# One more block on seven products, and three pieces of work moved to other engines, in a fused transformer layer on one core

## The chip, the cores and the metric

The kernel runs on one core of one Trainium2 chip. A core has a matrix engine (PE, or TensorE), three engines for element-wise work (DVE or VectorE, ACT or ScalarE, POOL or GpSimd) and queues that start transfers (SP, and one on each of the other engines). Each engine takes its own instructions strictly in the order in which they were written; where an instruction needs something from another engine, it waits on a semaphore, and everything behind it on its own engine waits too. The metric is the device time of one execution in microseconds; lower is better.

## The reference

One transformer layer without dropout, in float32, for two sequences (B = 2) of S = 1024 tokens of width D = 256, with a context of T = 154 rows of width 192 for each sequence:

```
h = layernorm(x, ln1);  x = attention(h, h) + x            # 16 heads of 64
h = layernorm(x, ln2);  x = attention(h, context) + x      # 16 heads of 64
h = layernorm(x, ln3)
p = h @ ff_w1 + ff_b1                                      # 256 -> 2 * 1024
a, gate = p[..., :1024], p[..., 1024:]
h = a * gelu(gate) @ ff_w2 + ff_b2                         # 1024 -> 256
return h + x
```

Only the last four lines, the gated layer, and the third layernorm are touched by the change.

## The kernel before

**The gated layer in blocks.** After the self attention (loop over `p`) and the cross attention (loop over `c`), a last loop over `k` runs the gated layer. The 2048 tokens are cut into `NPR` = 4 blocks ("pairs" in the code) of 512: blocks 0 and 1 are the first sequence, 2 and 3 the second. For each block the first projection is made in `NF` = 8 pieces of 128 hidden features, and each piece takes two steps: `gate_first` (even `k`) and `gate_second` (odd `k`), with a remainder, `gate_last`, that is issued inside the next `gate_first`. So block 0 is made in steps 0 to 15, block 1 in 16 to 31, block 2 in 32 to 47, block 3 in 48 to 63. The pieces are numbered n = k // 2.

**The first projection** is written as seven products in place of eight (a Strassen-Winograd scheme for 2x2 blocks), with sums of weights (`weight_sums`) and sums of tokens (`token_sums`) made on GpSimd beforehand. In each piece, PE makes 7 products of 128x256 into the PSUM tiles `pa`, `pb`, `pc`; ScalarE copies `pa` to `own[:, 0]` (L1097), VectorE adds it to the others (L1101, L1103, L1117, L1120, L1129), ScalarE makes the two GELUs (L1115, L1121), and GpSimd multiplies value and gate into `ub`, the two hidden tiles of a block (L1122, L1131; 256 tokens each, called j = 1 and j = 0). `pa` is written twice: by product 1 in `gate_first` and, accumulating, by product 2 in `gate_second`, which may not start before ScalarE has copied the first value out (L1097).

**The second projection** has two forms. Blocks in `FAST`, which is 1 to 3, take seven products too: `quick_tokens` makes sums of the hidden values (4 operations of 128x128 for each pair of feature pieces and each j, 32 a block, L1194 to L1197), `quick_weights` makes four sums of the second weight (128x512 each, L1179 to L1182), and `fast_sum` is one of the seven products, 4 matrix products of 128x128 for each j (L1217). Block 0 takes `sum_slot` instead: 32 plain matrix products of 128x256 (L1247). Either way the work goes into the list `sums`, from which each step of the loop takes two plain products or one `fast_sum`; the sums of hidden values go into the list `combos`, from which each step takes two. Results are added to the tokens `x` by VectorE (L1231, L1257; the first of the seven products also by GpSimd, L1226) and then stored to `out` by DMA.

**Where the sums live.** `hold_quick` takes the tile `quick` in the place of a big attention tile that the cross attention still reads until step 5. Before, it is called in step 18, with the weight sums put at the head of `combos`.

**The third layernorm of the second sequence** (`norm_beside("ff", B - 1)`, from step 7) runs beside the gated layer of the first: for each pair of token tiles, VectorE makes mean and variance (L242, L243), GpSimd makes `var` and `rstd` (L248, L252: `deviation`), VectorE makes `off` = -mean * rstd (L258), GpSimd writes the normalized tiles `xn` (L273), PE turns them (L286), and ScalarE writes them to `hT` (L301). There are four such pairs of tiles. Their tokens are not needed before block 2.

**The order** is written out by hand, piece by piece; the lines of one step of the loop stand in this order:

```
(gate_second if k % 2 else gate_first)(k // 2)      # 7 products a piece, with gate_last
...
fn, n = sums.pop(0)                                 # second projection, 2 or 1 a step
...
for _ in range(min(2, len(combos))): combos.pop(0)[1]()
run_work(0 if k == 1 else 1 + k % 2, k % 2)         # a step of the norm
```

Of the kernel before, what the change touches and what calls it, by code (L numbers as in the profile page):

```python
# [18 lines left out]
def tile_transformer_block(ctx: ExitStack, tc: tile.TileContext, a: dict, out: bass.AP):  # L19
    nc = tc.nc  # L20
# [3 lines left out]
    B, S, D = x.shape  # L24
# [27 lines left out]
    NF = DF // P  # L52
# [9 lines left out]
    small = ctx.enter_context(tc.tile_pool(name="small", bufs=4))  # L62
# [35 lines left out]
    for n in names:  # L98
        k = n_of[n]
# [68 lines left out]
    for n in names[2:]:  # L168
        own = rows[row_of[n] - n_cols:row_of[n] - n_cols + n_of[n], :]
# [53 lines left out]
    def norm_pieces(kind, b, first=False):  # L223

        ln = {"sa": "ln1", "ca": "ln2", "ff": "ln3"}[kind]
        g0, b0 = row_of[ln + "_g"], row_of[ln + "_b"]  # L230
        st = {}
        nh = NC if kind == "ff" else NH
        order = tile_order(kind)

        def stats(t):
            if t == 0:
                st["hT"] = hT[kind, b] = p2.tile(
                    [P, nh, NC * S // nh], F32, tag="hT", name=f"hT_{ln}_{b}")
            if t % 2 == 0:
                st["mv", t] = small.tile([P, 2, 2], F32, tag="mv", name=f"mv_{ln}_{b}_{t}")  # L240
            s6 = small.tile([P, 6], F32, tag="st", name=f"st_{ln}_{b}_{t}")
            nc.vector.bn_stats(s6, xt[b, order[t] // GT][:, order[t] % GT, :])  # L242
            nc.vector.bn_aggr(st["mv", t // 2 * 2][:, t % 2, :], s6)  # L243

        def deviation(t):
            mv = st["mv", t]
            var = small.tile([P, 2], F32, tag="var", name=f"var_{ln}_{b}_{t}")
            (nc.vector if first else nc.gpsimd).tensor_scalar(  # L248
                var, mv[:, :, 1], EPS, 1.0, op0=ALU.add, op1=ALU.mult
            )  # L250
            rstd = small.tile([P, 2], F32, tag="rstd", name=f"rstd_{ln}_{b}_{t}")
            nc.gpsimd.tensor_tensor(rstd, var, power, ALU.pow)  # L252
            st["rstd", t] = rstd

        def normalize(t):
            rstd = st["rstd", t]
            off = small.tile([P, 2], F32, tag="off", name=f"off_{ln}_{b}_{t}")
            nc.vector.scalar_tensor_tensor(  # L258
                off, st["mv", t][:, :, 0], -1.0, rstd, op0=ALU.mult, op1=ALU.mult
            )  # L260
            if narrow(kind, b) and not first:
                xn = st["hT"][:, :, t * P // 2:(t + 2) * P // 2].rearrange(
                    "p c (i d) -> p c i d", i=2)
                st["xn", t] = [xn[:, c].rearrange("p i d -> p (i d)") for c in range(nh)]
            else:
                xn = pp_.tile([P, nh, 2, D // nh], F32, tag="P", name=f"xn_{ln}_{b}_{t}")
                flat = xn.rearrange("p c i d -> p (c i d)")
                st["xn", t] = [flat[:, i * P:(i + 1) * P] for i in range(2 * D // P)]
            for i in range(2):
                xs = xt[b, order[t + i] // GT][:, order[t + i] % GT, :]  # L270
                xs, own = xs.rearrange("p (c d) -> p c d", c=nh), xn[:, :, i, :]
                if not narrow(kind, b) or first and i == 1:
                    nc.gpsimd.tensor_scalar(  # L273
                        own, xs, rstd[:, i:i + 1], off[:, i:i + 1], op0=ALU.mult, op1=ALU.add)
                else:
                    nc.scalar.activation(
                        own, xs, AF.Identity, bias=off[:, i:i + 1], scale=rstd[:, i:i + 1])

        def turn(t):

            n = 2 if first else 1
            bank = mm_tile if first and t == 2 else spare["bank"]
            ph = [bank(f"ph_{ln}_{b}_{t}_{i}") for i in range(n)]
            for i in range(2 * D // P):

                nc.tensor.transpose(  # L286
                    ph[i * n * P // (2 * D)][:, i % (2 * D // P // n) * P:][:, :P],
                    st["xn", t][i], ident)

            def store():  # L290
                k = NC * 2 * P // nh
                for c in range(nh):
                    own = st["hT"][:, c, t // 2 * k:(t // 2 + 1) * k]
                    turned = ph[c * n // nh][:, c % (nh // n) * k:][:, :k]
                    gain, shift = cols[:, g0 + c:g0 + c + 1], cols[:, b0 + c:b0 + c + 1]
                    if spare["turned"] or first and c < nh // 2:
                        nc.vector.tensor_scalar(
                            own, turned, gain, shift, op0=ALU.mult, op1=ALU.add
                        )
                    else:  # L300
                        nc.scalar.activation(own, turned, AF.Identity, bias=shift, scale=gain)  # L301

            return store

        return (
            [lambda t=t: stats(t) for t in range(NT)],
            *([lambda t=t, f=f: f(t) for t in range(0, NT, 2)] for f in (deviation, normalize, turn)),
        )

    def tile_order(kind):  # L310

        if kind == "ff":
# [457 lines left out]
    CG = [(t, min(TG, NT - t)) for t in range(0, NT, TG)]  # L770
# [224 lines left out]
    NPR = B * 2  # L995
    BT = S // 4
    FU = NPR * NF
    wsum, wh, ub, psum, pools = {}, {}, {}, {}, {}
# [144 lines left out]
                (lambda i=i, e=e: sum_slot(pair, i, e), 1) for i in range(2 * TF) for e in range(NF))  # L1143

    sums, summed, quick, combos, mixed = [], {}, {}, [], {}
    FAST = range(1, NPR)
    NHF = NF // 2

    def hold_quick():
# [22 lines left out]
    def quick_weights():  # L1172

        (b11, b12), (b21, b22) = (
            [w2[:, h::2, d * P:(d + 1) * P] for d in range(2)] for h in range(2))
        t1, t2, t3, t4 = (quick["w", i] for i in (1, 2, 3, 4))
        tt = nc.gpsimd.tensor_tensor
        return [
            lambda: tt(t1, b12, b11, ALU.subtract),  # L1179
            lambda: tt(t2, b22, t1, ALU.subtract),  # L1180
            lambda: tt(t3, b22, b12, ALU.subtract),
            lambda: tt(t4, b21, t2, ALU.subtract),  # L1182
        ]

    def quick_tokens(pair, j, c, engine=nc.gpsimd):

        u, own = ub[pair][j], quick["u", (2 * pair + j) % 4]
        (a11, a12), (a21, a22) = (
            [u[:, 2 * c + h, e * P:(e + 1) * P] for h in range(2)] for e in range(2))
        s1, s2, s4 = (own[:, i, c, :] for i in range(3))  # L1190
        tt = engine.tensor_tensor
        mixed[pair, j] = mixed.get((pair, j), 0) + 1
        return [
            lambda: tt(s1, a21, a22, ALU.add),  # L1194
            lambda: tt(s2, s1, a11, ALU.subtract),
            lambda: tt(a21, a11, a21, ALU.subtract),
            lambda: tt(s4, a12, s2, ALU.subtract),  # L1197
        ]

    def fast_sum(pair, j, g):  # L1200
# [63 lines left out]
    with tc.manual_schedule():  # L1264
# [59 lines left out]
        for p in range(SA):  # L1324
# [28 lines left out]
            if hg == LAG:  # L1353
                f = (ui - NPAIR // 2 - 1) * EC
# [108 lines left out]
        for k in range(2 * FU):  # L1463
            c = CA + k
            if k == 0:
                run_work(0, 0, n_sum=2)
            flush(adds)
            (gate_second if k % 2 else gate_first)(k // 2)
            flush(stores)
            flush(lates)  # L1470
            if k == 2 * len(CG) + 1:
                norm_beside("ff", B - 1)
            cross_drain(c)
            if k % 2:
                cross_weigh(c - 1 if k == len(CG) + 2 else c)
            cross_regroup(c)
            if k == len(CG) + 2:
                out_pieces("ca", B - 1, NQ - 1, out_order("ca"))
            if k % (2 * NF) == NF and k < 2 * FU - 2 * NF:
                token_sums(k // (2 * NF) + 1)  # L1480
            n_left = 2
            while n_left > 0 and sums:
                fn, n = sums.pop(0)
                n_left -= n
                run(fn)
            flush(stores)
            if k == 2 * NF + 2:
                hold_quick()
                combos[:0] = [(None, fn) for fn in quick_weights()]
            for _ in range(min(2, len(combos))):  # L1490
                combos.pop(0)[1]()
            run_work(0 if k == 1 else 1 + k % 2, k % 2)
            if later and (k <= len(CG) + 2 or k > 2 * NF):
                if k <= len(CG) + 2 or k % 2:
                    later.pop(0)()
# [39 lines left out]
```

## Time and profile before

| | us |
|---|---|
| time, median of 3 runs | 1072.13 (1070.64 to 1073.63) |
| the profiled execution, its own time | 1075.05 |
| its span, first to last instruction | 1073.2 |
| PE busy in the span | 1059.4 (99%) |
| VectorE, ScalarE, GpSimd busy in the span | 883.1, 646.9, 777.0 |
| first product of the gated layer starts at | 900.79 |

The profile is of one execution. A busy PE is not a PE at its peak: matrix products are pipelined, and their ends are modelled, so the distance from one start to the next says what a product costs. In float32 a matrix product shows as two records; "x4" of the plain second projection is two products. Times in the views are microseconds from the start of the span. A line such as L1097 is line 1097 of the kernel before.

### The profile page before, as it was taken

What the parts mean: (1) busy time and instruction counts of PE and PEld (TensorE: products, weight loads), DVE (VectorE), ACT (ScalarE), POOL (GpSimd) and SP (SyncE); (2) the same over time, 40 slices, a digit from 0 to 9 for tenths busy, and PEclk for the clock granted to TensorE, in tenths of its full rate; (3) what the DMA queues carried; (4) which work ended last, traced back from release to release, by engine and by line L of the source; (5) the groups of instructions that cost most, each with busy time, mean ns of one, the idle gap of its engine ahead of it and who ended that gap; (6) DMA issues with size and microseconds to landing.
All of it is one profiled execution on the core that took longest, in us unless ns stands there. A gap on an engine that the chain in (4) does not pass through costs nothing.

```text
span 1073.2 us, 48628 instructions
## 1 busy us (share of the span) xinstructions
PE 1059.4 (99%) x20196; PEld 716.2 (67%) x20196; DVE 883.1 (82%) x1321; ACT 646.9 (60%) x2096; POOL 777.0 (72%) x1652
## 2 busy tenths in 40 slices
PE   8999999999999999999999999999999999999998
PEld 6566777556556555555665665466766667788998
DVE  5789899998989989999999899968777887655554
ACT  5766677677666666676777666665566564342231
POOL 2677777778777777677777777776666876499884
PEclk9999999999999999999999999999999999999999
DMA  3132122121021121111111101125776545000000
GB/s 101 38 73 54 29 68 53 25 63 41 22 59 25 34 51 34 39 34 34 44 22 45 44 14 38 36 59 139 164 177 172 123 108 114 16 6 15 21 10 30
DMA packets 86045, 60.95 MB, mean 57 GB/s; under 512 B 32122, under 2 KB 74562, under 8 KB 85826
## 3 DMA queue, kind: packets, MB, share of 16 engines
q1 hardware_dynamic: 84450, 57.07, 22.1%
q8 instruction: 159, 2.61, 1.1%
q10 hardware_dynamic: 1376, 0.79, 0.2%
q14 instruction: 60, 0.49, 0.2%
HBM read 27.91 MB, written 2.10 MB: 28 GB/s over the span
## 4 chain that ended last, share of the span: by engine, by line
PE 74%; DMA 7%; SPq 6%; POOL 6%; DVE 2%; issue 2%; ACT 1%; POOLq 0%; DVEq 0%; ACTq 0%
PE s L526 14%; PE po L578 13%; DMA st<-st 7%; SPq L547 6%; PE py_ca L500 5%; PE py_sa L500 4%; PE poc L951 4%; PE pq_ca L369 4%; PE pq_sa L369 4%; PE pb L1072 4%; PE pk_sa L369 4%; PE pq L1217 3%; PE pv_sa L405 3%; POOL p L650 3%; PE sc L871 2%; PE pa L1072 2%
## 5 line engine op out<-in xcount | busy, mean ns | idle before, releaser
L650 POOL TENSOR_SCALAR p<-p,rd,ee 128x512 f32<-128x512 f32 x512 | 391.9, 771 | 80.0 <-DVE rd L640 79.6
L537 ACT ACTIVATE p<-s,st 128x512 f32<-128x512 f32 x512 | 345.5, 687 | 169.7 <-DVE st L712 164.5
L712 DVE TENSOR_REDUCE st<-s 128x2 f32<-128x1024 f32 x256 | 308.6, 1206 | 56.8 <-issue 17.3
L675 DVE STREAM_TRANSPOSE pT<-p 128x1024 f32<-128x1024 f32 x256 | 302.8, 1219 | 1.5 <-POOL p L650 1.2
L526 PE MATMUL s<-k_sa,q_sa 64*32 64x512 f32 x4096 | 257.8, 591 | 2.8 <-ACT p L537 2.0
L578 PE MATMUL po<-pT,held_v 64*32 64x256 f32 x8192 | 240.8, 376 | 0.7 <-DVE pT L675 0.6
L578 PEld LDWEIGHTS po<-pT,held_v 64*32 64x32 f32 x8192 | 182.5, 106 | 67.0 <-issue 26.0
L526 PEld LDWEIGHTS s<-k_sa,q_sa 64*32 64x32 f32 x4096 | 89.7, 106 | 93.1 <-issue 46.6
L888 ACT ACTIVATE p<-sc,neg 128x154 f32<-128x154 f32 x256 | 96.4, 405 | 78.9 <-DVE rden L896 75.0
L899 POOL TENSOR_SCALAR p<-p,rden 128x154 f32<-128x154 f32 x256 | 97.3, 406 | 51.8 <-DVE rden L896 51.5
L537 ACT ACTIVATION_READ_ACCUMULATOR p<-s,st 128x1 f32 x512 | 104.0, 203 | 0.0
L555 POOL TENSOR_TENSOR dd<-st 128x8 f32<-128x8 f32 x128 | 26.0, 203 | 82.4 <-DMA st<-st 80.6
L500 PE MATMUL py_sa<-sa_wo,o_sa 128*128 128x256 f32 x256 | 59.7, 386 | 1.0 <-ACT held_v L415 1.0
L500 PE MATMUL py_ca<-ca_wo,o_ca 128*128 128x256 f32 x256 | 60.2, 383 | 0.0
L877 DVE TENSOR_REDUCE neg<-sc 128x6 f32<-128x924 f32 (+1 forms) x48 | 47.8, 996 | 14.9 <-PE sc L871 14.9
L369 PE MATMUL pq_ca<-hT_ln,ca_wq 64*64 64x512 f32 (+1 forms) x544 | 59.1, 590 | 0.9 <-DMA ca_wq<-in_L_xattn_ca_wq_dram 0.8
L500 PEld LDWEIGHTS py_sa<-sa_wo,o_sa 128*128 128x128 f32 x256 | 47.3, 190 | 19.0 <-issue 5.2
L369 PE MATMUL pq_sa<-hT_ln,sa_wq 64*32 64x512 f32 (+1 forms) x976 | 57.8, 586 | 0.7 <-ACT held_v L415 0.7
L369 PE MATMUL pk_sa<-hT_ln,sa_wk 64*32 64x512 f32 x960 | 57.1, 590 | 0.2 <-ACT q_sa L384 0.2
L888 ACT ACTIVATION_READ_ACCUMULATOR p<-sc,neg 128x1 f32 x256 | 56.5, 221 | 0.0
L915 DVE STREAM_TRANSPOSE pT_ca<-p 128x480 f32<-128x480 f32 (+1 forms) x96 | 52.9, 587 | 0.9 <-POOL p L899 0.8
L405 PE MATMUL pv_sa<-sa_wv,hT_ln 64*32 64x256 f32 x1792 | 52.9, 376 | 0.0
(158 smaller groups left out, 1476.0 us busy)
## 6 DMA issues: line engine op xcount, KB each, us to landing
wf<-pT_ca SPq DMA_DIRECT2D x128, 128.0 KB, 2.4
st<-st SPq DMA_DIRECT2D x512, 1.0 KB, 2.0
held_v<-held_v SPq DMA_DIRECT2D x32, 256.0 KB, 4.0
sa_wq<-in_L_xattn_sa_wq_dram SPq DMA_DIRECT2D x32, 128.0 KB, 2.8
sa_wk<-in_L_xattn_sa_wk_dram SPq DMA_DIRECT2D x32, 128.0 KB, 3.6
sa_wv<-in_L_xattn_sa_wv_dram SPq DMA_DIRECT2D x16, 256.0 KB, 4.2
ca_wq<-in_L_xattn_ca_wq_dram SPq DMA_DIRECT2D x32, 128.0 KB, 3.1
wf<-in_L_xattn_ff_w_dram SPq DMA_DIRECT2D x12, 256.0 KB
```

The lines of the kernel that those rows point to most:

```text
L369: nc.tensor.matmul(pq[r][f:f + m, at:at + n], lhsT=wt[own, c, f:f + m], rhs=h[own, c, t0:t0 + n], start=(c == 0), stop=(c == NH - 1), tile ...
L405: nc.tensor.matmul(pv[r][f:f + KB, e * VC:(e + 1) * VC], lhsT=h[half, c, t0:t0 + KB], rhs=wt[half, c, :], start=(c == 0), stop=(c == NH - ...
L500: nc.tensor.matmul(py[:, e * D:(e + 1) * D], lhsT=o[:, i, (t + e) * P:(t + e + 1) * P], rhs=wo[kind][:, g * HP + i, :], start=(i == 0), st ...
L526: nc.tensor.matmul(sc[a4 * KB:(a4 + 1) * KB, j, :], lhsT=q[r, c:c + KB], rhs=k[r, h * HB:(h + 1) * HB], start=True, stop=True, tile_positi ...
L537: nc.scalar.activation(pr[:, j, :], sc[:, j, :], AF.Exp, bias=st[:, 0, 0, i, j:j + 1], accum_out=st[:, 0, 1, i, j:j + 1],)
L578: nc.tensor.matmul(po[a2][d:d + KB, :QH // 2], lhsT=v[e][r, t, d:d + KB], rhs=pT[r, d // DH * NK + n, :], start=(t == 0 and e == 0), stop= ...
L650: nc.gpsimd.tensor_scalar(pr[:, j, :], pr[:, j, :], own["rd"][:, c:c + 1], own["ee"][:, 0, c:c + 1], op0=ALU.mult, op1=ALU.mult,)
L675: nc.vector.transpose(halves[h][:, :, c:c + KB], slots[p]["p"][i].rearrange("p j (n k) -> p (j n) k", k=KB))
L712: nc.vector.tensor_reduce(st[:, 0, 0, i, :], sc[i], AX.X, ALU.max, negate=True)
L888: nc.scalar.activation(pr_[:, j, i, :T], sc[:, j, i * T:(i + 1) * T], AF.Exp, bias=neg[:, j, i:i + 1], accum_out=den[:, j, i:i + 1],)
L899: nc.gpsimd.tensor_scalar(pr_[:, j, i, :T], pr_[:, j, i, :T], rden[:, j, i:i + 1], 1.0, op0=ALU.mult, op1=ALU.mult,)
L1072: nc.tensor.matmul(into[:, :BT], lhsT=lhs, rhs=wh[pair][i], start=first, stop=True, skip_group_check=True)
```

## The change

Five edits:

1. `FAST` takes in block 0, so its second projection is made as 14 groups of four 128x128 products instead of 32 products of 128x256, with 32 more sums of hidden values.
2. `hold_quick` and the weight sums move from step 18 to step 6, and the weight sums from GpSimd to VectorE.
3. Steps 6 to 17 take three entries from `combos`, later ones two as before, earlier ones none.
4. In the third layernorm of the second sequence (`late`), VectorE makes -mean (`neg`) in `deviation`, and GpSimd multiplies it by `rstd` right behind making it; the VectorE instruction at L258 is gone there.
5. The normalized tiles of that layernorm are written by ScalarE instead of GpSimd.

```diff
+        late = kind == "ff" and b == B - 1
...
             nc.gpsimd.tensor_tensor(rstd, var, power, ALU.pow)
             st["rstd", t] = rstd
+            if late:
+                neg = small.tile([P, 2, 4], F32, tag="zz", name=f"neg_{ln}_{b}_{t}")[:, 0, :2]
+                nc.vector.tensor_scalar(neg, mv[:, :, 0], -1.0, 1.0, op0=ALU.mult, op1=ALU.mult)
+                off = st["off", t] = small.tile([P, 2], F32, tag="off", name=f"off_{ln}_{b}_{t}")
+                nc.gpsimd.tensor_tensor(off, neg, rstd, ALU.mult)
...
-            nc.vector.scalar_tensor_tensor(
-                off, st["mv", t][:, :, 0], -1.0, rstd, op0=ALU.mult, op1=ALU.mult
-            )
+            if late:
+                off = st["off", t]
+            else:
...
-                if not narrow(kind, b) or first and i == 1:
+                if kind == "ca" and not narrow(kind, b) or kind == "ff" and b == 0 or first and i == 1:
                     nc.gpsimd.tensor_scalar(
                         own, xs, rstd[:, i:i + 1], off[:, i:i + 1], op0=ALU.mult, op1=ALU.add)
                 else:
                     nc.scalar.activation(
                         own, xs, AF.Identity, bias=off[:, i:i + 1], scale=rstd[:, i:i + 1])
...
-    FAST = range(1, NPR)
+    FAST = range(NPR)
...
-        tt = nc.gpsimd.tensor_tensor
+        tt = nc.vector.tensor_tensor
         return [
             lambda: tt(t1, b12, b11, ALU.subtract),
             lambda: tt(t2, b22, t1, ALU.subtract),
...
-            if k == 2 * NF + 2:
+            if k == 2 * len(CG):
                 hold_quick()
                 combos[:0] = [(None, fn) for fn in quick_weights()]
-            for _ in range(min(2, len(combos))):
+            n_mix = 0 if k < 2 * len(CG) else 3 if k < 2 * NF + 2 else 2
+            for _ in range(min(n_mix, len(combos))):
                 combos.pop(0)[1]()
```

`len(CG)` is 3, so `2 * len(CG)` is step 6, and `2 * NF + 2` is step 18. In `quick_tokens` the views into `quick` are taken when the operation is issued rather than when it is listed, since block 0's are listed from step 4, before `quick` is held.

More of the change, by code (lines that the diff above doesn't have):

```diff
@@ L253, in deviation @@
             st["rstd", t] = rstd
+            if late:
[3 more added lines that the diff above has]
+                nc.gpsimd.tensor_tensor(off, neg, rstd, ALU.mult)
         def normalize(t):
             rstd = st["rstd", t]
-            off = small.tile([P, 2], F32, tag="off", name=f"off_{ln}_{b}_{t}")
-            nc.vector.scalar_tensor_tensor(
-                off, st["mv", t][:, :, 0], -1.0, rstd, op0=ALU.mult, op1=ALU.mult
-            )
+            if late:
+                off = st["off", t]
+            else:
+                off = small.tile([P, 2], F32, tag="off", name=f"off_{ln}_{b}_{t}")
+                nc.vector.scalar_tensor_tensor(
+                    off, st["mv", t][:, :, 0], -1.0, rstd, op0=ALU.mult, op1=ALU.mult
+                )
             if narrow(kind, b) and not first:
@@ L1185, in quick_tokens, with s @@
     def quick_tokens(pair, j, c, engine=nc.gpsimd):
-        u, own = ub[pair][j], quick["u", (2 * pair + j) % 4]
+        u = ub[pair][j]
         (a11, a12), (a21, a22) = (
             [u[:, 2 * c + h, e * P:(e + 1) * P] for h in range(2)] for e in range(2))
-        s1, s2, s4 = (own[:, i, c, :] for i in range(3))
         tt = engine.tensor_tensor
+        def s(i):
+            return quick["u", (2 * pair + j) % 4][:, (0, 1, None, 2)[i - 1], c, :]
         mixed[pair, j] = mixed.get((pair, j), 0) + 1
         return [
-            lambda: tt(s1, a21, a22, ALU.add),
-            lambda: tt(s2, s1, a11, ALU.subtract),
+            lambda: tt(s(1), a21, a22, ALU.add),
+            lambda: tt(s(2), s(1), a11, ALU.subtract),
             lambda: tt(a21, a11, a21, ALU.subtract),
-            lambda: tt(s4, a12, s2, ALU.subtract),
+            lambda: tt(s(4), a12, s(2), ALU.subtract),
         ]
```

## The prediction

> **What bounds the kernel now.** I read the page first, then the busy time by stretches, then the timeline of each engine from the first step of the gated layer on.
>
> ```profile
> span 1073.2 us, 48628 instructions
> ...
> PE 1059.4 (99%) x20196; PEld 716.2 (67%) x20196; DVE 883.1 (82%) x1321; ACT 646.9 (60%) x2096; POOL 777.0 (72%) x1652
> ```
>
> PE works in 99% of the span, so the kernel is as long as PE's list plus what PE waits. A change helps by shortening that list and hurts by making PE wait; other engines count only through such waits. The stretches (columns: length, PE, PE's weight loads, DVE, ACT, POOL) show where a wait is near:
>
> ```profile
> 928.90:946.00 17.10, 16.02 (x75) 12.59 (x74) 13.82 (x40) 7.07 (x17) 14.45 (x25) 1.00 0.00 1
> 946.00:984.00 38.00, 38.00 (x182) 33.46 (x181) 18.18 (x44) 12.74 (x29) 35.29 (x58) 1.00 0.03 11
> ```
>
> Steps 8 to 17 of the gated layer lie at 929.36 to 949.11. There GpSimd is busy 14.45 of 17.1 us, and PE already waits a little. After 946 PE never waits, and GpSimd is at 93%. The clock is 1.00, so no price hides a throttle.
>
> **The change part by part.** *Block 0 on seven products.* One step's share of the second projection, plain (948.25) and in seven products (984.95), with the start of what follows:
>
> ```profile
> 948.25 1.03 PE L1247 MATMUL pf<-wf,held_v 128*128 128x256 f32 x4
> 949.11 0.60 PE L286 MATMUL ph_ln<-ident,xn_ln 128*128 128x128 f32 x4
> ...
> 984.95 1.05 PE L1217 MATMUL pq<-wf,u 128*128 128x128 f32 x8
> 985.84 0.60 PE L1072 MATMUL pa<-hT_ln,wf 128*128 128x256 f32 x2
> ```
>
> Plain: two products in 0.86 us, 32 products, 16 steps: 13.8 us. Seven: four products in 0.89 us, 56 products, 14 steps: 12.5 us. PE's list loses 1.3 us. That is the whole gain on PE: an eighth of the columns of one block.
>
> *What GpSimd gets for it.* 32 more sums of hidden values, 24 of them issued in steps 7 to 15, ahead of things that others wait for; each `off` is one more small operation. In return the four weight sums (at 952.6 to 958.4 before) and eight `xn` tiles (four pairs of 1.1 us) leave it.
>
> ```profile
> 928.88 0.73 POOL L1122 TENSOR_TENSOR kT<-own 128x256 f32<-128x256 f32 x1 [3.63 <-ACT own L1121]
> 930.99 0.73 POOL L1131 TENSOR_TENSOR held_v<-own 128x256 f32<-128x256 f32 x1 [1.38 <-DVE own L1129]
> 931.67 0.73 POOL L1055 TENSOR_TENSOR hs<-hT_ln 128x256 f32<-128x256 f32 x1
> ...
> 934.54 0.72 POOL L1122 TENSOR_TENSOR kT<-own 128x256 f32<-128x256 f32 x1
> 935.33 0.19 POOL L248 TENSOR_SCALAR var_ln<-mv_ln 128x2 f32<-128x2 f32 x1
> 935.61 0.71 POOL L252 TENSOR_TENSOR rstd_ln<-var_ln,power 128x2 f32<-128x2 f32 x1
> 936.28 0.73 POOL L1131 TENSOR_TENSOR held_v<-own 128x256 f32<-128x256 f32 x1
> ...
> 959.85 0.45 POOL L1194 TENSOR_TENSOR quick<-u 128x128 f32<-128x128 f32 x1
> 960.38 0.46 POOL L1195 TENSOR_TENSOR quick<-quick,u 128x128 f32<-128x128 f32 x1
> 960.79 0.73 POOL L1122 TENSOR_TENSOR u<-own 128x256 f32<-128x256 f32 x1
> 961.48 0.46 POOL L1196 TENSOR_TENSOR u<-u 128x128 f32<-128x128 f32 x1
> 961.89 0.46 POOL L1197 TENSOR_TENSOR quick<-u,quick 128x128 f32<-128x128 f32 x1
> 962.30 0.73 POOL L326 TENSOR_TENSOR x<-x,ff_b 128x256 f32<-128x256 f32 x1
> ```
>
> Start to start, a multiplication takes 0.69 us (930.99 to 931.67), `var` and `rstd` together 0.95 (935.33 to 936.28), four sums of hidden values 0.94 + 0.82 = 1.76, so 0.44 each (0.41 to 0.53 for a single one). `off` has no row; its nearest are 0.19 (`var`, same size) and 0.71 (the power). I take 0.22, since a plain multiplication of two columns is nearer to `var`.
>
> Two sums go into the idle 1.38 us ahead of 930.99 (928.88 + 0.69 + 0.94 = 930.5), so up to 934.54 nothing moves. From there to the end of the last multiplication of block 0 (n = 7), GpSimd now has 8 multiplications (5.5), 22 sums (9.7), 4 pairs of `var` and `rstd` (3.8) and 4 `off` (0.9): 19.9 us, ending at 954.4. The last product of step 17 (group g = 1) reads that multiplication's result. Before, PE was at that place at about 948.9: the last quarter of the slot 948.25 to 949.11. So PE comes there 5.5 us late. At 0.41 to 0.53 a sum and 0.19 to 0.71 an `off`, it is 4.7 to 9.4.
>
> *How PE is held on the way.* The normalized tiles now stand in ScalarE's line, and wait there for `off` with everything behind them:
>
> ```profile
> 936.88 0.35 ACT L1097 COPY own<-pa 128x256 f32<-128x256 f32 x1
> ...
> 937.53 0.59 PE L1072 MATMUL pa<-hT_ln,wf 128*128 128x256 f32 x2
> ...
> 938.86 0.70 PE L1072 MATMUL pb<-hT_ln,wf 128*128 128x256 f32 x2 [0.74 <-DVE own L1101]
> ...
> L276 ACT ACTIVATE xn_ln<-x,off_ln,rstd_ln 128x256 f32<-128x256 f32 x4 | 2.4, 600 | 3.8 <-DVE off_ln L258 3.8
> ```
>
> The first `off` comes after 6 sums, a multiplication, `var`, `rstd` and itself: 934.54 + 2.6 + 0.7 + 0.95 + 0.22 = 939.0. Two tiles of 0.60, then the copy at L1097 (0.35), end near 940.5. Product 2 of n = 6, at 937.53 before, must wait for that copy: PE stands about 3 us there, where before it lost 0.74 one product later. VectorE's L1101 waits for the same copy. The next two `off` come every 5.2 us (two multiplications 1.4, six sums 2.6, 0.95, 0.22), while two steps on PE take some 3.5 to 5 us. These holds are no further terms: they are how the 5.5 us build up.
>
> *Weight sums on VectorE*, between L1103 and L507 in step 6 (three) and behind step 7 (one):
>
> ```profile
> 924.81 0.42 DVE L1103 TENSOR_TENSOR own<-pc,own 128x256 f32<-128x256 f32 x1
> 926.54 0.69 DVE L507 TENSOR_TENSOR x<-py_ca,x 128x512 f32<-128x512 f32 x1 [1.30 <-PE py_ca L500]
> 927.40 0.48 DVE L1117 SCALAR_TENSOR_TENSOR own<-pb,cols,own 128x256 f32<-128x256 f32 x1 [0.17 <-PE pb L1072]
> ...
> L1179 POOL TENSOR_TENSOR quick<-wf 128x512 f32<-128x512 f32 x1 | 1.3, 1272 | 0.0
> ```
>
> The row nearest in engine and size is L507, 0.69 us; the bounds are 0.42 (half the size) and 1.27 (the same sum on GpSimd). Three take 2.1 us, and 1.3 are idle. So L507 and the chain behind it (L1117, L1120, ScalarE's GELU, the multiplication at 928.88) come some 0.5 us later, 0 to 2.4 by the bounds. This moves GpSimd's start, so it adds: 0.5.
>
> *What comes after.* Past step 18 GpSimd has 5.1 us of weight sums less, and catches up. In step 33 block 1's last product waits for the multiplication of n = 15:
>
> ```profile
> 985.80 0.72 POOL L1131 TENSOR_TENSOR u<-own 128x256 f32<-128x256 f32 x1
> ...
> 987.14 1.05 PE L1217 MATMUL pq<-wf,u 128*128 128x128 f32 x8
> ...
> L1226 POOL TENSOR_TENSOR x<-x,ends 128x384 f32<-128x384 f32 x4 | 4.0, 996 | 0.0
> ```
>
> Before, the result was there at 986.5 and read at about 987.8, 1.3 us to spare. PE now gets there 1.3 us sooner relative to GpSimd (steps 30 and 31 are empty), and GpSimd has one more L1226 (1.0) on the way once it runs level. I add 0.5, between 0 and 1.0.
>
> *At nothing:* `neg`, twelve more result adds less four on VectorE (18.18 of 38 us busy), two more copies on ScalarE (12.74 of 38), and the stores of block 0, for which nothing waits. They stay hidden while those engines idle half the time.
>
> *Sum:* 5.5 + 0.5 + 0.5 - 1.3 = +5.2 us. Against the profiled execution: 1075.05 (1.85 outside the span) + 5.2 = 1080.2. That execution lies 2.9 above the median shown; on the median it is 1072.13 + 5.2 = 1077.3. The bounds together give +2.9 (4.7 + 0 + 0 - 1.3 = 3.4, less 0.5 for small waits before that go) to +11.5.
>
> **The rivals.**
>
> [...] Where VectorE and GpSimd both work, VectorE's instructions with two inputs in SBUF stretch:
>
> ```profile
> 936.35 0.68 DVE L258 SCALAR_TENSOR_TENSOR off_ln<-mv_ln,rstd_ln 128x2 f32<-128x2 f32 x1
> ...
> 948.79 0.15 DVE L258 SCALAR_TENSOR_TENSOR off_ln<-mv_ln,rstd_ln 128x2 f32<-128x2 f32 x1
> ...
> L1196 DVE TENSOR_TENSOR u<-u 128x128 f32<-128x128 f32 x1 | 0.8, 812 | 0.0
> L1197 DVE TENSOR_TENSOR quick<-u,quick 128x128 f32<-128x128 f32 x1 | 0.3, 279 | 0.0
> ```
>
> The same small instruction took 0.15 or 0.68, the same sum 0.28 or 0.81: about 0.53 more each. If all four weight sums pay that, 2.1 us join the VectorE term: +7.3, 1079.4. Against it: GpSimd idles 3.63 us ahead of 928.88, just when they run. Chance 0.12. [...]
>
> *GpSimd's lag is taken up* (not slower). `own` has seven buffers, and no multiplication is read by PE before step 16. If `off` came as soon as before, and the tokens' sums found idle time, only the gain would be left: -1.3, and PE's 0.74 at 938.86 gone: -2.0, 1070.1. It decides if `off` is there by 937. For it: GpSimd idles 2.65 of 17.1 us. Against it: 6 sums stand ahead of the first `off`, 22 in all, 9.7 us. Chance 0.09.
>
> *The same holds, but smaller*: sums at 0.41, the first waits partly inside those of before: 0 to +3.2, about 1074. Chance 0.17.
>
> **How the numbers follow.** The forecast has 0.62, with +3.2 to +9, 1075.3 to 1081. The range 1073 to 1081 leaves out the second rival and part of the third below, the far end of the first above. Differences under 0.3%, 3.2 us, are about what a measurement of this kernel can't tell from none. Slower: 0.62 + 0.12 = 0.74, of which I give 0.03 to the third case: 0.71. Within: the third rival, that 0.03 and most of the second: 0.24. Faster by 3.2 us would take more than all that PE waits there plus the 1.3: 0.05.
>
> **What would show it.** Right: ScalarE's first `xn` tile waiting for GpSimd near 939; PE standing 2 to 4 us before product 2 of n = 6; GpSimd without a gap from 931 to 954; step 17's group waiting for GpSimd; slots of 0.89 us, 14 of them. Wrong: `off` there before 938, PE without waits in steps 12 to 17, or weight sums on VectorE above 1.2 us.

## The result and the profile after

The changed kernel took 1079.39 us (median of 6 runs, 1076.49 to 1081.16), the kernel before in the same comparison 1071.81 (6 runs, 1070.64 to 1073.63). The ratio is 1.006, with a 95% interval of 1.0046 to 1.0075: slower by 4.9 to 8.0 us. The profiled execution of the changed kernel took 1079.61 us, against 1075.05 before.

The page of the changed kernel, its span and the busy time of the engines:

```profile
span 1077.6 us, 48783 instructions
...
PE 1060.0 (98%) x20244; PEld 731.9 (68%) x20244; DVE 886.9 (82%) x1333; ACT 650.4 (60%) x2106; POOL 785.0 (73%) x1678
```

PE's busy time is the same as before within 0.6 us, and the span is 4.4 longer: what came is nearly all waiting. Two executions also differ ahead of the gated layer, so I measure from its first product:

```profile
899.43 0.59 PE L1081 MATMUL pa<-hT_ln,wf 128*128 128x256 f32 x2
```

From there to the end of the span it is 1077.6 - 899.43 = 178.17 us, and was 1073.2 - 900.79 = 172.41: +5.76. This "stage" is the measure used for every run below. The same two stretches as before (length, PE, PE's weight loads, DVE, ACT, POOL, PE's clock):

```profile
928.90:946.00 17.10, 13.80 (x56) 10.37 (x55) 11.21 (x34) 7.27 (x17) 15.91 (x34) 0.90 0.00 0
946.00:984.00 38.00, 36.26 (x226) 32.95 (x225) 19.30 (x49) 15.02 (x35) 34.38 (x65) 1.00 0.04 12
```

In the first, PE falls from 16.02 to 13.80 us while GpSimd rises from 14.45 to 15.91; in the second PE, which never waited, lacks 1.74 us. The view of waits from 925 to 1000 us names for PE (in total, times, longest):

```profile
PE pa L1081 <- ACT own L1106: 3.0, 3, 2.6
PE pq L1229 <- POOL held_v L1140: 1.5, 1, 1.5
PE pb L1081 <- DVE own L1110: 0.5, 1, 0.5
PE pq L1229 <- POOL u L1140: 0.4, 1, 0.4
```

Before, PE had 0.74 and 0.21 there. Now it is 5.4 us in all. (L1081 is the old L1072, L1106 the copy at the old L1097, L1110 the old L1101, L1140 the old L1131, L1229 the old L1217.) Who stands behind the 2.6 is read by going from engine to engine. GpSimd's timeline, with the first and the last part of the list that the prediction counts:

```profile
932.76 0.73 POOL L1067 TENSOR_TENSOR hs<-hT_ln,hs 128x256 f32<-128x256 f32 x1
933.45 0.46 POOL L1208 TENSOR_TENSOR held_v<-held_v 128x128 f32<-128x128 f32 x1
...
936.20 0.46 POOL L1209 TENSOR_TENSOR quick<-kT,quick 128x128 f32<-128x128 f32 x1
936.74 0.19 POOL L249 TENSOR_SCALAR var_ln<-mv_ln 128x2 f32<-128x2 f32 x1
937.01 0.71 POOL L253 TENSOR_TENSOR rstd_ln<-var_ln,power 128x2 f32<-128x2 f32 x1
937.80 0.20 POOL L259 TENSOR_TENSOR off_ln<-neg_ln,rstd_ln 128x2 f32<-128x2 f32 x1
...
952.88 0.20 POOL L259 TENSOR_TENSOR off_ln<-neg_ln,rstd_ln 128x2 f32<-128x2 f32 x1
953.03 0.73 POOL L1140 TENSOR_TENSOR held_v<-own 128x256 f32<-128x256 f32 x1
953.71 1.01 POOL L1238 TENSOR_TENSOR x<-x,ends 128x384 f32<-128x384 f32 x1
```

ScalarE's, where the first pair of normalized tiles stands ahead of the copy:

```profile
938.03 1.09 ACT L285 ACTIVATE xn_ln<-x,off_ln,rstd_ln 128x256 f32<-128x256 f32 x2 [1.93 <-POOL off_ln L259]
939.03 0.35 ACT L1106 COPY own<-pa 128x256 f32<-128x256 f32 x1
```

PE's, at the copy and at step 17:

```profile
936.23 0.59 PE L1081 MATMUL pc<-hs,w1s 128*128 128x256 f32 x2
939.43 1.22 PE L1081 MATMUL pa<-hT_ln,wf 128*128 128x256 f32 x2 [2.61 <-ACT own L1106]
940.45 1.06 PE L1081 MATMUL pb<-hT_ln,wf 128*128 128x256 f32 x2
941.30 1.06 PE L1081 MATMUL pc<-hT_ln,w1s 128*128 128x256 f32 x2
942.15 0.74 PE L295 MATMUL ph_ln<-ident,xn_ln 128*128 128x128 f32 x4
942.74 0.60 PE L1081 MATMUL pa<-hT_ln,wf 128*128 128x256 f32 x2
...
950.03 0.70 PE L1081 MATMUL pa<-hT_ln,wf 128*128 128x256 f32 x2 [0.20 <-ACT own L1106]
...
953.81 0.49 PE L1229 MATMUL pq<-wf,held_v 128*128 128x128 f32 x2 [1.52 <-POOL held_v L1140]
954.14 0.60 PE L295 MATMUL ph_ln<-ident,xn_ln 128*128 128x128 f32 x4
...
956.30 1.05 PE L1229 MATMUL pq<-quick 128*128 128x128 f32 x8
957.19 0.60 PE L1081 MATMUL pa<-hT_ln,wf 128*128 128x256 f32 x2
```

The first `off` ends at 938.00, ScalarE starts its tiles at 938.03 after 1.93 idle, copies at 939.03, and PE goes on at 939.43. Then, at step 17, PE waits 1.52 for the multiplication that GpSimd starts at 953.03. The products right behind the long pause are 1.02 and 0.85 us apart instead of 0.43, at a granted clock of 0.54 (939.40 to 942.70); the last section takes this up.

### The profile page after: what moved, and what is told of

The parts are those of the page before. It is cut to its first block, busy times and chain, and to the rows that moved or that the text cites. A ratio compares the mean times of both kernels' runs of the same rounds, so it can differ in the third digit from the quotient of the medians.

```text
span 1077.6 us, 48783 instructions
## 1 busy us (share of the span) xinstructions
PE 1060.0 (98%) x20244; PEld 731.9 (68%) x20244; DVE 886.9 (82%) x1333; ACT 650.4 (60%) x2106; POOL 785.0 (73%) x1678
## 4 chain that ended last, share of the span: by engine, by line
PE 76%; POOL 7%; DMA 6%; SPq 5%; DVE 2%; issue 2%; ACT 1%; POOLq 0%; ACTq 0%; DVEq 0%
PE s L535 16%; PE po L587 15%; PE py_ca L509 5%; PE py_sa L509 5%; PE pk_sa L378 5%; PE pq_sa L378 4%; DMA st<-st 4%; SPq L556 4%; PE pq L1229 4%; PE poc L960 4%; PE pq_ca L378 3%; PE pv_sa L414 3%; PE pb L1081 3%; PE sc L880 2%; PE pa L1081 2%
## 5 line engine op out<-in xcount | busy, mean ns | idle before, releaser
L587 PEld LDWEIGHTS po<-pT,held_v 64*32 64x32 f32 x8192 | 186.5, 106 | 63.7 <-issue 22.9
L535 PEld LDWEIGHTS s<-k_sa,q_sa 64*32 64x32 f32 x4096 | 95.5, 106 | 88.8 <-issue 41.8
L509 PEld LDWEIGHTS py_ca<-ca_wo,o_ca 128*128 128x128 f32 x256 | 47.3, 190 | 8.2 <-issue 1.9
```

Source lines behind the costliest of these rows:

```text
L509: nc.tensor.matmul(py[:, e * D:(e + 1) * D], lhsT=o[:, i, (t + e) * P:(t + e + 1) * P], rhs=wo[kind][:, g * HP + i, :], start=(i == 0), st ...
L535: nc.tensor.matmul(sc[a4 * KB:(a4 + 1) * KB, j, :], lhsT=q[r, c:c + KB], rhs=k[r, h * HB:(h + 1) * HB], start=True, stop=True, tile_positi ...
L587: nc.tensor.matmul(po[a2][d:d + KB, :QH // 2], lhsT=v[e][r, t, d:d + KB], rhs=pT[r, d // DH * NK + n, :], start=(t == 0 and e == 0), stop= ...
```

## The experiments

Ten kernels, in three sets, each set timed in turn with the kernel before, on a chip of its own: before took 1075.29 us in the first set (e1 to e4), 1073.59 in the second (e5 to e8), 1074.87 in the third (e9, e10). Where an expectation names a time in us, it stands on the 1071.8 of the first comparison; what is compared is the ratio and the stage. Diffs are against the changed kernel. The letters in the expectations are theories; G is that of the prediction: GpSimd's list ahead of step 17. A stage is read from one traced execution. By the timed ratios e1, e8 and e9 are clear of the change; the intervals of e2 to e7 and of e10 overlap that of the change or of its repeat e5, so what tells those apart is one trace each.

| run | ratio to before (95%) | first product, end of span | stage | GpSimd's last multiplication ends |
|---|---|---|---|---|
| before | | 900.79, 1073.2 | 172.41 | 47.43 |
| the change | 1.006 (1.0046 to 1.0075) | 899.43, 1077.6 | 178.17 | 54.33 |
| e1_block0_plain | 1.0001 (0.999 to 1.0012) | 902.82, 1075.7 | 172.88 | 47.49 |
| e2_norm_back | 1.0069 (1.0047 to 1.0091) | 899.06, 1079.3 | 180.24 | 56.48 |
| e3_tiles_later | 1.0063 (1.0044 to 1.0082) | 901.16, 1079.7 | 178.54 | 54.27 |
| e4_weights_gpsimd | 1.0058 (1.0037 to 1.0079) | 899.25, 1077.9 | 178.65 | 54.90 |
| e5_change_again | 1.0044 (1.0027 to 1.006) | 896.78, 1074.8 | 178.02 | 54.26 |
| e6_half_vector | 1.0033 (1.0019 to 1.0046) | 898.46, 1073.1 | 174.64 | 50.03 |
| e7_late_start | 1.0045 (1.0029 to 1.0061) | 898.76, 1075.4 | 176.64 | 54.28 |
| e8_spread | 1.0004 (0.9994 to 1.0014) | 902.91, 1075.4 | 172.49 | 50.10 |
| e9_weights_first | 0.9994 (0.9981 to 1.0006) | 899.37, 1071.2 | 171.83 | 49.39 |
| e10_offsets_gpsimd | 1.0021 (1.0005 to 1.0037) | 903.13, 1076.4 | 173.27 | 49.38 |

The last column says where GpSimd ends the multiplication that step 17 reads (n = 7, j = 0), in us after the stage's first product. Against the change it moves by +2.15 in e2, +0.57 in e4 and -4.30 in e6, and the stage by +2.07, +0.48 and -3.53. In e3, e5 and e7 it stays within 0.1, and of these only e7, where PE reads it two steps later, has a shorter stage.

**e1: block 0 stays plain; everything else of the change remains.**

```diff
-    FAST = range(NPR)
+    FAST = range(1, NPR)
```

> The changed kernel with block 0's second projection left as 32 plain products; the weight sums stay on VectorE in steps 6 and 7, and the norm's offsets and tiles stay on GpSimd and ScalarE. Theory G (the 24 sums of hidden values that GpSimd takes in steps 7 to 15 set the pace up to step 17): they are gone, so the time is within 0 to +1.5 us of before (1071.8), and GpSimd is not on PE's path at step 17. [...] Theory S (the loss is that ScalarE's normalized tiles wait for GpSimd and hold the copy of pa): the offsets come some 3 us sooner without the sums, so +0 to +1.5 as well; this run does not tell S from G.

The ratio is 1.0001, and the stage 0.47 above that of before. PE's longest waits are those known from before:

```profile
937.35 0.70 PE L1081 MATMUL pb<-hT_ln,wf 128*128 128x256 f32 x2 [0.48 <-DVE own L1110]
...
940.78 0.70 PE L1081 MATMUL pa<-hT_ln,wf 128*128 128x256 f32 x2 [0.57 <-ACT own L1106]
```

So all but 0.5 us of the loss comes with block 0's seven products. The moved norm work and the weight sums on VectorE cost nothing that the timing shows, and at most these 0.5 us, as long as GpSimd has no sums of block 0.

**e2: the third layernorm as before (offsets on VectorE, tiles on GpSimd), the rest as changed.**

```diff
-        late = kind == "ff" and b == B - 1
+        late = False
...
-                if kind == "ca" and not narrow(kind, b) or kind == "ff" and b == 0 or first and i == 1:
+                if not narrow(kind, b) or first and i == 1:
```

> The changed kernel with the norm as before: offsets on VectorE, normalized tiles on GpSimd; block 0 still takes seven products and the weight sums stay on VectorE. Theory S: ScalarE's copy of pa is no longer held, so PE passes n = 6 without the 2.6 us wait and the time falls by 2.5 us or more against the change, to 1077 or less. Theory G: GpSimd's list up to the last multiplication of block 0 grows by three pairs of tiles (3.2 us) and loses four offsets (0.9), so it ends some 2 us later, and the time rises by 1 to 3 us against the change, to 1080 or more.

The stage is 2.1 us longer than the change's. PE waits longer, and for others:

```profile
939.87 0.70 PE L1081 MATMUL pb<-hT_ln,wf 128*128 128x256 f32 x2 [3.33 <-DVE own L1110]
...
943.08 1.44 PE L295 MATMUL ph_ln<-ident,xn_ln 128*128 128x128 f32 x4 [1.99 <-POOL xn_ln L282]
```

The tiles on ScalarE are thus no cause of the loss, although ScalarE's wait for `off` is the row one sees first. They take work off GpSimd and soften it. GpSimd's last multiplication ends at 954.82 + 0.72, 2.15 us later in the stage than in the change, which matches the 2.1 that the stage is longer:

```profile
954.82 0.72 POOL L1140 TENSOR_TENSOR held_v<-own 128x256 f32<-128x256 f32 x1
```

(PE's clock was low behind these pauses too: 0.63 from 939.90 to 943.20 and 0.50 from there to 946.50.)

**e3: tiles and turns of that norm one norm step later**, so that ScalarE does not reach its tiles before `off` is there.

```diff
-        for fns, first in ((turn, 3), (stats, 0), (deviation, 1), (normalize, 2)):
+        more = int(kind == "ff" and b == B - 1)
+        for fns, first in ((turn, 3 + more), (stats, 0), (deviation, 1), (normalize, 2 + more)):
...
-        for k in range(NT // n + 3):
+        for k in range(NT // n + 3 + more):
```

> The changed kernel with the normalized tiles (and their turning on PE) issued one norm step, that is two steps of the loop, later, so ScalarE no longer stands waiting for an offset ahead of the copy of pa; GpSimd's list is the same. Theory S: the 2.6 us wait at product 2 of n = 6 goes and with it 2.5 us or more: 1077 or less. Theory G: the wait moves to step 16 or 17, where PE then stands 3 to 5 us in all for the multiplication of n = 7, and the time stays within 1 us of the change. Theory C (after a pause PE runs for some 3 us at about half the clock, and that costs time of its own): with the one long pause now right at the end of GpSimd's chain, the slow products come after it and are no longer covered, so +1 to +1.5 us on top of the change.

The stage stays (178.54 to 178.17). The pause moved to step 16, and is named after GpSimd itself:

```profile
951.03 0.79 PE L1230 MATMUL pq<-wf,held_v 128*128 128x128 f32 x2 [3.72 <-POOL held_v L1141]
```

PE's wait of 2.6 for ScalarE's copy was only the place where GpSimd's lag first showed. Freed of it, PE runs ahead and waits 4.1 us for the multiplications (3.72, and 0.40 at step 17). GpSimd's last one ends 54.27 us into the stage, in the change 54.33:

```profile
954.71 0.72 POOL L1141 TENSOR_TENSOR held_v<-own 128x256 f32<-128x256 f32 x1
```

Theory C did not come true: PE's clock was low behind the pause, 0.53 from 951.20 to 954.50, but the stage is 0.37 longer and not 1 to 1.5. The wait of 0.40 at step 17 comes after the slow products, so these were covered once more.

**e4: the four weight sums back on GpSimd.**

```diff
-        tt = nc.vector.tensor_tensor
+        tt = nc.gpsimd.tensor_tensor
```

> The changed kernel with only the four weight sums put back on GpSimd, still in steps 6 and 7. [...] Theory G: three of the four (3.8 us) fall into GpSimd's idle time ahead of the multiplication in step 8 (5.6 and 3.9 us idle there), the fourth (1.3) partly delays its chain, while VectorE's chain comes 0.3 us sooner: within 1 us of the change.

The stage is 178.65, 0.48 above the change's: their place on VectorE does not make the loss. The first wait grows from 2.61 to 3.39:

```profile
939.85 0.70 PE L1081 MATMUL pa<-hT_ln,wf 128*128 128x256 f32 x2 [3.39 <-ACT own L1106]
```

**e5: the change once more**, beside e6 to e8 on their chip.

> The change as it is, beside the three variants on the same chip. Theory G (block 0's 24 sums of hidden values and the four offs on GpSimd, ahead of the multiplication that step 17 reads, hold PE): ratio 1.005 to 1.0075, stage from the first gate product to the end of the span 177.5 to 179 us, PE waits near 2.6 us before product 2 of n = 6 and 1.5 us at step 17. It is the measure for the variants: stages are compared with its stage.

Its stage, 178.02, repeats the 178.17 of the other chip within 0.15, and so do its waits (2.59 and 1.50). The ratio, 1.0044, lies just below the range that was expected; its interval meets that of the first comparison.

**e6: block 0's sums for j = 1 on VectorE**, 12 of those ahead of step 17.

```diff
-                engine = nc.vector if n == FU - 1 and j else nc.gpsimd
+                engine = nc.vector if (n == FU - 1 or pair == 0) and j else nc.gpsimd
```

> Half of block 0's sums of hidden values (those of j = 1, 12 of the 24 ahead of step 17) go to VectorE. Theory G: GpSimd loses 12 x 0.44 = 5.3 us of its list, so its last multiplication for step 17 is no longer late by more than about 1 us; the wait at step 17 (1.5) goes, the first off comes some 1.3 us sooner, and the hold before product 2 of n = 6 shrinks from 2.6 to about 1.3. Stage 2 to 4.5 us shorter than the change's, ratio to before 1.001 to 1.004. Rival V (VectorE and GpSimd contend, 0.8 us a sum instead of 0.28, and VectorE becomes what PE waits for): PE's waits are named after VectorE's own at L1110, and the stage is within 1 us of the change's or longer, ratio 1.005 or more.

The stage falls by 3.4 us against e5, within what G expected, and the wait at step 17 is gone. The timed ratio shows less (1.0033 to 1.0044): the traced execution, 1074.84 us, is the fastest of twelve whose median is 1077.76, and what sets it apart is taken up in the last section. The hold before product 2 of n = 6 is 0.57 us, where G expected 1.3. But 2.2 above before remain, and there V has a part in it: PE's longest wait now comes one piece earlier and is named after VectorE, whose line there is

```profile
931.26 0.81 DVE L1208 TENSOR_TENSOR kT<-kT 128x128 f32<-128x128 f32 x1
931.99 0.81 DVE L1209 TENSOR_TENSOR quick<-kT,quick 128x128 f32<-128x128 f32 x1
...
934.50 0.41 DVE L1110 TENSOR_TENSOR own<-pb,own 128x256 f32<-128x256 f32 x1
...
939.67 0.28 DVE L1208 TENSOR_TENSOR kT<-kT 128x128 f32<-128x128 f32 x1
```

and PE's

```profile
934.97 0.70 PE L1081 MATMUL pb<-hT_ln,wf 128*128 128x256 f32 x2 [2.45 <-DVE own L1110]
```

The same sum took 0.81 us once and 0.28 later. The slow ones stand ahead of the addition at 934.50 that PE waits for.

**e7: block 0's products two steps later** (two empty entries ahead of them).

```diff
+            if pair == 0:
+                sums.extend((lambda: None, 2) for _ in range(2))
```

> Block 0's products start two steps later (at step 18 instead of 16; steps 30 and 31 were empty). No sum is taken from GpSimd. Theory G: only the last wait, at step 17, moves to where GpSimd has finished; two slots of 0.89 stand behind it, so the wait of 1.5 goes and the stage is 1 to 1.5 us shorter than the change's; the wait of 2.6 before product 2 of n = 6 and the low clock behind it stay, and now show in the time as far as the wait at step 17 covered them. Rival C (the pause and the low clock behind it are a loss of their own, and the wait at step 17 is only what GpSimd has left over): stage within 0.5 us of the change's.

The stage is 1.38 us shorter than e5's, as G said, though in the traced execution the low clock that G counted on did not come (1.00 from 938.70 to 942.00); the timed ratio (1.0045 to 1.0044) does not show it. What was not expected is that the waits before the copies grow:

```profile
938.74 0.70 PE L1081 MATMUL pa<-hT_ln,wf 128*128 128x256 f32 x2 [2.59 <-ACT own L1106]
...
944.15 0.70 PE L1081 MATMUL pa<-hT_ln,wf 128*128 128x256 f32 x2 [1.60 <-ACT own L1106]
...
949.32 0.70 PE L1081 MATMUL pa<-hT_ln,wf 128*128 128x256 f32 x2 [1.36 <-ACT own L1106]
```

In the change the second and third wait were 0.22 and 0.20. Yet PE reaches the third of these products at the same distance from the stage's first: 949.32 - 898.76 = 50.56 here, 950.03 - 899.43 = 50.60 in the change. Whether PE comes there early and waits, or late, GpSimd's list decides when it goes on.

**e8: an attempt to keep the gain.** Block 0's sums are spread (one entry a step up to step 13, then three, those of j = 0 first), the products of blocks 0 to 2 start two steps later, and the additions of `ff_b2` go to VectorE.

```diff
-            nc.gpsimd.tensor_tensor(xs, xs, bias[bo], ALU.add)
+            (nc.vector if kind == "ff" else nc.gpsimd).tensor_tensor(xs, xs, bias[bo], ALU.add)
...
+            if pair < NPR - 1:
+                combos.sort(key=lambda e: e[0] or (-1, 0))
...
+            if pair < NPR - 1:
+                sums.extend((lambda: None, 2) for _ in range(2))
...
-            n_mix = 0 if k < 2 * len(CG) else 3 if k < 2 * NF + 2 else 2
+            n_mix = 0 if k < 2 * len(CG) else 1 if k < 2 * NF - 2 else 3 if k < 3 * NF + 4 else 2
```

> A version meant to keep the shorter PE list without GpSimd on PE's path: the sums of block 0 go one a step between steps 7 and 13 and three a step after that, those of j = 0 first; all blocks' products but the last's start two steps later; the additions of the layer's last offset (L335) are on VectorE. Theory G: up to step 15 GpSimd has about 8 sums (3.5 us) less ahead of the offs, so PE's waits in steps 12 to 17 fall to less than 1 us in all, and what is left is the shorter list: stage 0.5 to 1.3 us shorter than that of before, 5 to 7 shorter than the change's, ratio to before 0.9985 to 1.0. Rival V: with the additions on VectorE the results are late for PE, and the stage is 1 us or more longer than before's.

The stage is 172.49, that of before (172.41), and not 0.5 to 1.3 below it: 5.5 us of the change's loss are gone, the shorter list's gain is not there. PE still has two waits, 1.31 for VectorE's L1110 and 0.57. The weight sums now go one a step into steps 6 to 9, beside GpSimd's sums of gate inputs, which stretch from 0.73 to:

```profile
933.80 1.22 POOL L1064 TENSOR_TENSOR hs<-hT_ln 128x256 f32<-128x256 f32 x1
935.09 1.25 POOL L1065 TENSOR_TENSOR hs<-hT_ln,hs 128x256 f32<-128x256 f32 x1
```

**e9: as e8, with all four weight sums in step 6 and the sums of hidden values from step 10 on.**

```diff
-            n_mix = 0 if k < 2 * len(CG) else 3 if k < 2 * NF + 2 else 2
+            n_mix = (0 if k < 2 * len(CG) else 4 if k == 2 * len(CG) else 0 if k < 10
+                     else 1 if k < 2 * NF - 2 else 3 if k < 3 * NF + 4 else 2)
```

> As the spread version (e8_spread), but all four weight sums are issued in step 6, where VectorE waits for TensorE, none in steps 7 to 9, and the sums of hidden values begin in step 10. Theory G (what is left in the spread version's stage, 172.49 us against 172.41 before, is VectorE's own line: three weight sums of 0.68 between the instructions that TensorE's next product reads, with GpSimd's sums of gate inputs at 1.22 instead of 0.72 beside them): TensorE's wait of 1.31 for VectorE's own falls to below 0.6, GpSimd's sums of gate inputs (L1064, L1065) take 0.72 to 0.8, and the stage is 171.2 to 172.2, 0.2 to 1.2 us below that of before; ratio 0.998 to 1.0. Rival R (the first sums are not it; every layout with block 0 on seven products loses its 1.3 us again in small waits): stage 172.3 or more, ratio 1.0 to 1.002.

As G said: the wait for VectorE falls to 0.48, L1064 takes 0.73 again, and the stage is 171.83, 0.58 below before.

```profile
933.91 0.70 PE L1081 MATMUL pb<-hT_ln,wf 128*128 128x256 f32 x2 [0.48 <-DVE own L1110]
...
937.34 0.70 PE L1081 MATMUL pa<-hT_ln,wf 128*128 128x256 f32 x2 [0.57 <-ACT own L1106]
```

Its time, 1074.07 against 1074.87, has an interval (0.9981 to 1.0006) that holds 1. It is the best version of block 0 in seven products here, 6.3 us of stage below the change, but not shown to be faster than before.

**e10: as e9, with the additions of `ff_b2` left on GpSimd** (e8's first edit undone).

> As the version before it (e9_weights_first), but the additions of the layer's last offset (L335) stay on GpSimd. Theory G: 16 additions of 0.69 a block stand again between GpSimd's multiplications and sums from about 957 us on, where GpSimd is at over 90%; up to step 17 nothing differs, and later PE waits for GpSimd by 0 to 1.5 us in all, so the stage is 0 to 1.5 us longer than that version's. Rival: the additions on VectorE cost as much as they save, and the stage is the same within 0.3 or shorter.

The stage is 1.44 longer than e9's, at the upper end of what G gave. (The 16 additions are those of all blocks, four to a block, not 16 a block as the expectation has it.) Up to step 17 PE waits as in e9; then a result is late, because VectorE waits for GpSimd's addition to the same tokens. PE's row, then VectorE's:

```profile
978.25 1.16 PE L1233 MATMUL pq<-quick,kT 128*128 128x128 f32 x8 [0.84 <-DVE x L1247]
```

```profile
977.91 0.29 DVE L1247 TENSOR_TENSOR x<-pq,x 128x128 f32<-128x128 f32 x1 [2.65 <-POOL x L1242]
```

That wait is 0.84 of the 1.44; no wait of the trace names the rest. So GpSimd's load can hold PE past step 17 too, once the first part is spread out.

## Why the prediction was right, point by point

The forecast was 1077.3 us, 5.2 above the median shown; measured were 1079.39, which is 4.9 to 8.0 above before in the comparison (6.4 by the ratio) and 5.76 in the traces. The range of 1073 to 1081 holds it. The four terms as the traces show them are 5.87 + 0.27 + 0.41 - 1.04 = 5.51 of the 5.76; the errors of the single terms, up to 0.4, go both ways and cancel in part.

*GpSimd's list, +5.5.* Right, and slightly short. From the first sum behind the sums of gate inputs (933.45) to the end of the last multiplication (953.03 + 0.69) it took 20.27 us, forecast 19.9. From start to start an `off` took 0.15 where 0.22 was taken, but `var` and `rstd` together 1.06 where 0.95 was (936.74, 937.80 and 937.95). The second and third `off`, at 943.22 and 948.40, came 5.42 and 5.18 us behind the one before, forecast 5.2. Of the missing 0.4 some 0.25 are sums (single ones took 0.41 to 0.54 from start to start) and 0.14 the four groups of `var`, `rstd` and `off`. At the end of step 17's slot the change was behind by (954.14 - 899.43) - (949.11 - 900.79) = 6.39 us, where list and weight sums together had 6.0.

*The holds on the way.* Right in place and size: the first `off` was forecast at 939.0 - 900.79 = 38.2 us after the stage's first product and was there at 938.00 - 899.43 = 38.6; PE stood 2.61 us before product 2 of n = 6, forecast about 3. That these holds are not terms of their own was a claim of the prediction, and e3 shows it: take the first away and the time comes back at the next. In e7, where no low clock slows PE, the second wait is 1.38 longer, about the 1.4 that PE saves.

*Weight sums on VectorE, +0.5.* Right in sign and within its bounds. (The prediction's own rows give 2.07 - 1.30, less the 0.17 that L1117 had waited, so 0.6 rather than 0.5.) Two of their rows, with L516 (the old L507) behind them, and GpSimd's first multiplication:

```profile
924.55 0.69 DVE L1189 TENSOR_TENSOR quick<-wf,quick 128x512 f32<-128x512 f32 x1
925.16 0.69 DVE L1190 TENSOR_TENSOR quick<-wf 128x512 f32<-128x512 f32 x1
925.76 0.68 DVE L516 TENSOR_TENSOR x<-py_ca,x 128x512 f32<-128x512 f32 x1
```

```profile
927.79 0.72 POOL L1131 TENSOR_TENSOR kT<-own 128x256 f32<-128x256 f32 x1 [3.91 <-ACT own L1130]
```

Each took 0.68 or 0.69, as forecast. GpSimd came to its first sum 34.02 us after the stage's start instead of 33.75: +0.27.

*VectorE beside GpSimd.* The first rival fell: no weight sum was stretched (0.68 or 0.69 us each), and GpSimd idled 3.91 us beside them. e4, with the sums on GpSimd, was no faster. The stretch itself is there, though, in places where both engines work at once: 0.81 against 0.28 in e6 for one and the same line (the prediction's rows with these times were two different sums), 1.22 against 0.73 in e8. It went in both directions. In e6 VectorE was stretched, and GpSimd's sum had started first, at 931.15 against 931.26; in e8 GpSimd was, and VectorE's sums had started first, at 933.75 and 935.07 against 933.80 and 935.09. Before, VectorE's `off` took 0.68 and 0.67 where a multiplication on GpSimd had started 0.07 and 0.09 ahead of it, and 0.15 where GpSimd idled (948.79). What makes the two hold each other up no run shows.

*Step 33, +0.5.* It was 0.41, for the multiplication that the prediction named (one row of PE's waits above, `u` at L1140).

*PE's list, -1.3.* The slots are 0.89 us (956.30 to 957.19), as forecast. From the end of step 17's slot to the end of the span it was 1077.6 - 954.14 = 123.46 us, before 1073.2 - 949.11 = 124.09: -0.63. With the 0.41 of step 33 taken out that is -1.04, so the gain came but for some 0.3 that the two traces do not settle.

*The other rivals.* That GpSimd's lag is taken up needed `off` by 937 in the trace before, 36.2 us into the stage; it came at 38.6, and the gain alone was not seen. It took the further edits of e8 and e9 to come near it, and even then 0.58 us were seen in the stage and not the 2.0 of that rival. The same holds but smaller, 0 to 3.2, fell too: the stage is 5.76 longer.

*Not foreseen:* the drop of PE's clock after the pause, to 0.54 over 3.30 us, and that in the change it would cost nothing.

## What to carry to other kernels

An edit that shortens the busiest engine's list by 1.3 us can be paid for with 9.7 us of small operations on an engine that looks a quarter idle; count that engine's list between the two fixed points (what it starts from, and what the busy engine reads next), not its share of the span. The wait that one sees first, here ScalarE's for `off`, need not be the cause: when it was taken away (e3), the same time came back at the next meeting of the two engines, and only operations taken from or put later on GpSimd's list (e1, e6, e8 to e10) shortened the stage by more than the 1.4 us of e7. In these runs the place for VectorE's weight sums was where GpSimd idled: the four took 0.68 or 0.69 us there in the change, and where two of them ran beside GpSimd's own sums (e8), those took 1.22 and 1.25 instead of 0.73.

## What the runs showed of the hardware that was not expected

PE's granted clock fell to 0.50 for some 3.4 us at the end of the pause (939.1 to 942.5, seen in windows of 0.2 us). The window in the changed kernel, with PE's granted clock third from the end:

```profile
939.40:942.70 3.30, 3.27 (x10) 2.60 (x11) 1.54 (x4) 0.47 (x1) 3.06 (x8) 0.54 0.00 0
```

The products there are 1.02, 0.85 and 0.85 us apart. The same pause in e7, 2.59 us, was not followed by it (1.00):

```profile
938.70:942.00 3.30, 3.26 (x17) 2.69 (x18) 2.69 (x10) 0.98 (x2) 3.06 (x8) 1.00 0.00 0
```

From the pause's end to the fifth group of rows it took 942.74 - 939.43 = 3.31 us in the change and 940.66 - 938.74 = 1.92 in e7: 1.4 us lost to the clock. It cost nothing in the end, since both reach the product at the third copy (950.03 and 949.32) at 50.6 us after the stage's start; the slow products only fill time that PE would have waited for GpSimd. The executions of the change agree: the two with a mean granted clock of 1.0 took 1079.07 and 1079.56 us, the four with 0.998 took 1076.49 to 1081.16.

That it is free is not shown for other kernels. In e6 the four executions at a mean clock of 1.0, the traced one among them, took 1075.8 us in the mean and the eight below it 1078.6; in e7 the three at 1.0, again with the traced one, took 1077.6 and the four below 1079.2. The slower ones were not traced, so where their clock fell stays open.

Of the pauses in the gated layer, 3.72 (e3), 3.39 (e4), 3.33 with 1.99 close behind (e2), 2.61 (the change) and 2.59 (e5) were followed by a low clock, 2.59 (e7) and 2.45 (e6) were not. So a pause of about 2.6 us went either way in these runs. Nor does a low mean clock need such a pause in the gated layer: the traced executions of e8 and e10 have a mean of 0.998, with 1.00 in every window read from 895 us (e8) and 930 us (e10) to 1060, and their longest waits there are 1.31 and 0.84 us. Where their clock fell is not shown here.

How long the clock stayed low in the other runs is an estimate from the mean clocks of their windows, with the 0.50 of the change while it lasts: 3.4 us in e3 (2.70 us at 0.95 and 3.30 at 0.53), in e4 (2.10 at 0.63 and 3.00 at 0.69) and in e5 (1.60 each at 0.72, 0.50 and 0.71), and 6.9 in e2 with its two pauses (3.30 at 0.63, 3.30 at 0.50 and 3.50 at 0.84). What sets this length, and why equal pauses differ, the runs do not show.

A smaller surprise is `neg`, which the prediction had at nothing: a VectorE instruction on 128x2 with one input took 0.16 us at its shortest and 0.43 at its longest, 0.35 in the mean of its four. It stayed hidden: no wait of PE is named after it.

```profile
L257 DVE TENSOR_SCALAR neg_ln<-mv_ln 128x2 f32<-128x2 f32 x4 | 1.4, 349 | 0.0
```
